# A fused attention, attention and mixture-of-experts kernel: six of eight expert matrices moved to the third phase, and its one-hot products in bf16

## The chip, the core and the metric

The kernel runs on one core of one Trainium2 chip. The metric is the device time of one execution in microseconds (us). The kernel before the change took 5177.51 us (median of 3 runs, 5173.71 to 5183.84).

A core has five engines that work side by side, each through its own queue in order: PE (TensorE, matrix products), DVE (VectorE), ACT (ScalarE), POOL (GpSimd) and SP (SyncE, which here only starts transfers). They wait for each other by semaphores. PE writes its results to PSUM[...].

## The reference, cut to what matters

A layer over x of 8 x 1024 tokens of 256 numbers: a first attention within each token (16 heads of 64, causal over the 64), a residual and a norm; then a second block with an ordinary attention over the leading axis, a norm giving y, and a mixture of experts:

```python
cap = S // E                                   # 8192 tokens, 8 experts: 1024
gates = softmax(xf @ wg); idx = argmax(gates)
loc = place of the token within its expert     # by a cumulative sum
keep = loc < cap
slot = idx * cap + loc
disp[slot] = xf
h = einsum('ecd,edf->ecf', disp, w1) + b1      # 256 -> 1024, no function between
y = einsum('ecf,efd->ecd', h, w2) + b2         # 1024 -> 256
out = where(keep, gate * y[slot], 0)
```

and two more norms. As nothing stands between w1 and w2, an expert is one matrix w1 w2 (256 x 256) and one bias row b1 w2 + b2. The kernel makes both itself, from inputs of 1 MB each per expert.

## The kernel before, in words

All work is in fp32 and in an order written out by hand (`tc.manual_schedule()`): each engine gets its instructions in the order in which the program calls them. There are three phases.

**Phase a** (`phase_a`) is the attention within tokens, over 64 tiles of 128 tokens. It takes the first 4332 us or so and isn't touched.

**Phase b** (`phase_b`, L540 on) is the attention over the leading axis and the choice of the expert. The tokens go in eight groups j of 1024. A group has four parts n. In part n, PE makes the `scores` of one half of the heads and one half of the positions; ACT turns them into `weights`; PE turns the result (`turn_s`) and makes the weighted sum of the part before. Between these steps the kernel calls the jobs of a list, `fills(j)`: the projections of the next group (`turn_x`, `project_qk`, `project_v`), and of the group before its `output`, `normal`, `turn_y`, `logits`, `exps` and `choice`. `some(k)` takes k jobs off the list, so the place of a job in the list decides what it stands between.

One kind of job is `expert(j, piece)` (L832): in group j the matrix of expert j is made, a quarter in each part. A piece is four fp32 products of 128x128 by 128x256 (L841), which accumulate in one PSUM bank `pw` over the four pieces, and two steps of DVE (L849) that add b1 times w2 to `acc`, from which the bias row comes. After the fourth piece ACT copies the bank to `w12` (L853). Each part's 256 KB of w1 and of w2 are started by SP at the start of the part (`load_expert`, L824), from a pool with two buffers each. SP's queue also holds the stores of finished rows (L765, L817) and the loads of x (L597).

`normal` makes y and y plus the bias of the second norm: two steps of DVE (L758), then three passes of POOL (L761, L762) to the tile `yx`; `turn_y` on PE (L773) waits for that. In group 7 there is no next group, and the expert's first piece stands earlier in the list.

**Phase c** (`phase_c`, L948 on) begins with the routing: PE counts with triangular and full matrices of ones (L975, L977, and `p_over`, L993), DVE works out each token's slot (split in `high` and `low`). Then one-hot products invert the list: for 8 columns of tokens at a time, DVE makes `is_low` (128 x 8 x 128) and `is_high` (128 x 8 x 64), POOL multiplies `is_high` with the token's number (L1056), and PE sums 64 products into `p_tok` (L1059). DVE casts the sum to `token`, the number of the token in each slot (L1063). The first row gather needs it.

Then come rounds r from -2 to 17 over 16 groups q of 512 slots. In round r, by the list `order`: POOL starts the gathers of q = r + 2 (L1083); ACT makes `roots`; PE turns the rows of q = r + 1 (`turned`, L1097) and ACT copies them to `xT` (L1101); PE makes the products of q = r + 1 with `w12` of its expert (`product`, L1108 and L1118); DVE adds them up for q = r (`blend`, L1147, L1135); ACT norms (`normed`, L1186: n of q = r - 1, o of q = r - 2); DVE adds the residual for q = r - 1 (`join`, L971); POOL scatters o of q = r - 2 to the output (L1204). Expert e is needed by the products of q = 2e and 2e + 1.

Of the kernel before, what the change touches and what calls it, by code (L numbers as in the profile page):

```python
# [24 lines left out]
FP = mybir.dt.float32  # L25
BF = mybir.dt.bfloat16
I32 = mybir.dt.int32
# [6 lines left out]
P = 128  # L34
D = 256
# [7 lines left out]
FC = FF // P  # L43
CAP = L * N // E
RW = 2 * D + 1
EPS = 1e-5
MASKED = 1e30

@with_exitstack
def fused_kernel(ctx: ExitStack, tc: tile.TileContext, a: dict, out: bass.AP):  # L50
    nc = tc.nc

    const = ctx.enter_context(tc.tile_pool(name="const", bufs=1))
    small = ctx.enter_context(tc.tile_pool(name="small", bufs=4))

    ident = const.tile([P, P], FP, name="ident")
    make_identity(nc, ident)
    mhalf = const.tile([P, 1], FP, name="mhalf")
    nc.gpsimd.memset(mhalf, -0.5)

    dram = ctx.enter_context(tc.tile_pool(name="dram", bufs=1, space=bass.MemoryType.DRAM))
    x1_d = dram.tile([L * N, D], FP, name="x1_d")
    rows_d = dram.tile([L * N, RW], FP, name="rows_d")

    def norm_scalars(r):

        st = small.tile([P, 6], FP, name="st")
        nc.vector.bn_stats(out=st, in_=r)
        mv = small.tile([P, 2], FP, name="mv")
        nc.vector.bn_aggr(out=mv, in_=st)  # L70
# [17 lines left out]
    constants(nc, late, keep)  # L88
    nc.scalar.dma_start(keep["gain"], a["ln2_g"].partition_broadcast(P))
    phase_b(tc, a, ident, x1_d, rows_d, keep, norm_scalars)  # L90
    phase_c(tc, ident, rows_d, keep, out)


def constants(nc, late, keep):
# [445 lines left out]
def phase_b(tc, a, ident, x1_d, rows_d, keep, norm_scalars):  # L540
# [8 lines left out]
    with (  # L549
# [271 lines left out]
            nc.vector.tensor_reduce(red_v[:, j], lg, AX.X, ALU.max)  # L821
            nc.vector.tensor_tensor(hot_v[:, j], rank, over_experts(red_v[:, j]), ALU.is_equal)

        def load_expert(e, piece):  # L824
            f0 = piece * 2 * P
            w1 = kp.tile([P, 2, D], FP, name="w1")
            nc.sync.dma_start(w1, a["w1T"][e, f0 : f0 + 2 * P, :].rearrange("(c p) d -> p c d", p=P))
            w2 = kp.tile([P, 2, D], FP, name="w2")
            nc.sync.dma_start(w2, a["w2"][e, f0 : f0 + 2 * P, :].rearrange("(c p) d -> p c d", p=P))
            G["we", e, piece] = w1, w2  # L830

        def expert(e, piece):  # L832

            w1, w2 = G["we", e, piece]
            if piece == 0:
                G["pw", e] = p1.tile([P, 512], FP, name="pw")
            pw = G["pw", e]
            for i in range(2):
                fc = piece * 2 + i
                for d in range(DC):  # L840
                    nc.tensor.matmul(  # L841
                        pw[:, d * D : (d + 1) * D],
                        w1[:, i, d * P : (d + 1) * P],
                        w2[:, i, :],
                        start=fc == 0 and d == 0,
                        stop=fc == FC - 1,
                        skip_group_check=True,
                    )
                nc.vector.scalar_tensor_tensor(  # L849
                    acc[:, e, :], w2[:, i, :], b1[:, fc, e : e + 1], acc[:, e, :], ALU.mult, ALU.add  # L850
                )
            if piece == 3:
                nc.scalar.copy(w12[:, :, e, :], pw.rearrange("p (c d) -> p c d", c=DC))  # L853

        def fills(j):

# [2 lines left out]
            nxt, prv = j + 1, j - 1  # L859
            N = nxt < NJ  # L860
            O = prv >= 0
            X = 0 <= j < NJ

            def put(part, ok, fn, *args):
                if ok:
# [2 lines left out]
            put(0, N, turn_x, nxt, 0)  # L868
            put(0, N, turn_x, nxt, 2)
            put(0, N, turn_x, nxt, 4)  # L870
            put(0, not N and X, expert, j, 0)
            put(0, O, output, prv, 0)
            put(0, N, turn_x, nxt, 6)
            put(0, O, output, prv, 2)
            put(0, N and X, expert, j, 0)
            put(0, O, normal, prv, 0)
            put(0, N, project_qk, nxt, 0, 0, 0)
            put(1, O, normal, prv, 2)
# [3 lines left out]
            put(1, O, logits, prv, 0)  # L882
            put(1, O, normal, prv, 4)
            put(1, O, turn_y, prv, 2)
            put(1, X, expert, j, 1)
# [8 lines left out]
            put(2, X, expert, j, 2)  # L894
# [8 lines left out]
            put(3, X, expert, j, 3)  # L903
            put(3, N, project_qk, nxt, 1, 1, 0)
            put(3, O, choice, prv)
            put(3, N, project_qk, nxt, 1, 1, 1)
            return o

        before = None
        for j in range(-1, NJ + 1):  # L910
# [4 lines left out]
            for n in range(4):  # L915
                work = list(parts[n])

                def some(k):
                    for _ in range(k):

                        if work and not (n == 0 and before and work[0][0] is output):
                            fn, *args = work.pop(0)
                            fn(*args)

                live = 0 <= j < NJ
                if live:
                    load_expert(j, n)
                    c, ib = divmod(n, 2)
                    st = scores(j, c, ib)
                    some(1)  # L930
                    weights(st, 0)
                if before:
                    sT = turn_s(before[3])
                    some(2 if live else 0)
                if live:
                    weights(st, 1)
                    normed(st)
                if before:
# [9 lines left out]
def phase_c(tc, ident, rows_d, keep, out):  # L948


    nc = tc.nc
# [3 lines left out]
    with (  # L955
        tc.tile_pool(name="cone", bufs=1) as op,
        tc.tile_pool(name="cwork", bufs=4) as kp,
        tc.tile_pool(name="crow", bufs=5) as gp,
        tc.tile_pool(name="cnorm", bufs=3) as np_,
        tc.tile_pool(name="cp", bufs=3, space=PSUM) as pp,  # L960
        tc.tile_pool(name="cq", bufs=4, space=PSUM) as pq,
        tc.manual_schedule(),
    ):
# [5 lines left out]

        def tt(o, x, y, alu):  # L970
            nc.vector.tensor_tensor(o, x, y, alu)  # L971


        p_in = pp.tile([P, 512], FP, name="ps")
# [17 lines left out]
        p_over = pp.tile([P, 512], FP, name="ps")  # L992
        nc.tensor.matmul(p_over[:, :NT], keep["before"], over, start=True, stop=True)  # L993
        nc.tensor.matmul(p_over[:, NT : 2 * NT], keep["ones"], over, start=True, stop=True)
        tt(slot, slot, loc, ALU.add)

        count = new("count", (P, E))
# [36 lines left out]
        nc.vector.scalar_tensor_tensor(low, high, -float(P), slot, ALU.mult, ALU.add)  # L1034


        K = 8
        p_tok = pq.tile([P, 512], FP, name="pr")
        column = keep["column"]
        for k in range(NT // K):  # L1040
            ts = slice(K * k, K * k + K)
            is_low = np_.tile([P, K, P], FP, name="is_low")
            tt(
                is_low,
                low[:, ts, None].to_broadcast([P, K, P]),
                column[:, None, :].to_broadcast([P, K, P]),
                ALU.is_equal,
            )
            is_high = np_.tile([P, K, NT], FP, name="is_high")
            tt(  # L1050
                is_high,
                high[:, ts, None].to_broadcast([P, K, NT]),
                column[:, None, :NT].to_broadcast([P, K, NT]),
                ALU.is_equal,
            )
            nc.gpsimd.tensor_tensor(is_high, is_high, place[:, ts, None].to_broadcast([P, K, NT]), ALU.mult)  # L1056
            for i in range(K):
                t = K * k + i
                nc.tensor.matmul(  # L1059
                    p_tok[:, :NT], is_low[:, i, :], is_high[:, i, :], start=t == 0, stop=t == NT - 1  # L1060
                )
        token = op.tile([P, NT], I32, name="token")
        nc.vector.tensor_copy(token, p_tok[:, :NT])  # L1063

        valid = new("valid", (P, E, ST))
        tt(
            valid,
# [2 lines left out]
            ALU.is_lt,  # L1070
        )
        valid = valid.rearrange("p e s -> p (e s)")

        st = {}
        moments = {}
# [123 lines left out]
        def scatter(q, i):  # L1199
# [21 lines left out]
            (turned, -1, 1),  # L1221
            (product, -1, 0),
            (product, -1, 1),
            (blend, 0, 0),
            (scales, None),
            (normed, 1, 0),
# [9 lines left out]
        for r in range(-2, NQ + 2):  # L1236
            for fn, d, *args in order:
                if d is None:
                    fn(r)
# [48 lines left out]
```

## Time and profile before

| what | value |
|---|---|
| median of 3 runs | 5177.51 us |
| the profiled execution, its own time | 5169.03 us |
| its span, first to last instruction | 5167.3 us |
| PE busy over the span | 4927.5 us, 95% |
| DVE, ACT, POOL busy | 59%, 65%, 65% |
| mean granted clock of PE | 0.976 |
| expert products, L841 | 256 instructions, 67.2 us busy |
| bias steps, L849 | 64 instructions, 43.2 us busy |
| one-hot products, L1059 | 128 instructions, 27.6 us busy |
| POOL's multiply, L1056 | 8 instructions, 10.1 us busy |

An fp32 product counts as two instructions of PE in the profile, so 128 products of L841 are 256. A row of the timeline gives the start in us from the start of the span, the time that it lasts, the engine (PEld is PE's loading of weights), the line, the operation, output and inputs with shapes, how many instructions were merged (x8), and in brackets the idle time of the engine just before it and what ended that. The granted clock is the share of full speed at which PE was allowed to run. Several rows of one line follow each other closely: an instruction may start before the end of the one before it, so the price of one in a row is the distance of the starts.

### The profile page before, as it was taken

The page shows a single profiled execution, that of the slowest core. Times are in us where ns is not written, and L with a number is a line of the kernel's source. Part 1 is how long each engine was busy: PE and PEld are TensorE (multiplying, and loading weights), DVE is VectorE, ACT ScalarE, POOL GpSimd, SP SyncE. Part 2 cuts the span into 40 slices and gives each one's busy share as a digit, 9 for nine tenths or more (in the row PEclk, how much of TensorE's full clock was granted, in tenths as well). Part 3 has the DMA queues.
Part 4 walks back from the last instruction along what each step waited for, and adds up shares of the span by engine and source line. Part 5 has one row for each costly group of instructions (what it writes and reads, how often), then busy time and mean ns, then how long its engine had stood idle before and what let it go on. Part 6 is the DMA issues. An engine that isn't in the chain of part 4 may idle for free. (4 is left out here: it accounts for less than half of the span.)

```text
span 5167.3 us, 189788 instructions
## 1 busy us (share of the span) xinstructions
PE 4927.5 (95%) x79752; PEld 3334.8 (65%) x79752; DVE 3065.7 (59%) x6079; ACT 3348.2 (65%) x4067; POOL 3377.5 (65%) x7022
## 2 busy tenths in 40 slices
PE   7999999999999999999999999999999997998765
PEld 4666666666666666666666666666666664666553
DVE  5656666566656666656656566656666652555467
ACT  5777777777777777777777777777777773443224
POOL 5767666767676776667667767676776763344446
PEclk9999999999999999999999999999999998999877
DMA  2222222222222222222222222222222222233223
GB/s 76 47 48 49 47 49 48 47 47 48 49 47 47 48 49 46 48 48 49 47 48 49 47 48 49 48 47 48 48 49 46 48 47 72 62 82 82 62 81 120
DMA packets 569357, 280.00 MB, mean 54 GB/s; under 512 B 395057, under 2 KB 520113, under 8 KB 568497
## 3 DMA queue, kind: packets, MB, share of 16 engines
q1 hardware_dynamic: 360018, 105.22, 10.8%
q0 software_dynamic: 204800, 159.82, 10.5%
q8 instruction: 623, 10.21, 0.9%
q10 hardware_dynamic: 3680, 2.83, 0.2%
q14 instruction: 236, 1.93, 0.1%
HBM read 66.02 MB, written 33.59 MB: 19 GB/s over the span
## 5 line engine op out<-in xcount | busy, mean ns | idle before, releaser
L358 ACT ACTIVATE e<-pair 128x1024 f32<-128x1024 f32 x3072 | 2977.3, 1021 | 1235.5 <-PE pair L342 1235.5
L402 POOL DMA_DIRECT2D nd<-S x4096 | 1948.9, 484 | 612.0 <-DVE S L392 418.8
L342 PE MATMUL pair<-R,L 32*128 32x128 f32 (+1 forms) x32768 | 1606.2, 322 | 2.2 <-POOL event L313 2.1
L392 DVE COPY S<-sum 128x512 f32<-128x512 f32 x1024 | 706.6, 690 | 1469.2 <-PE sum L381 1138.7
L342 PEld LDWEIGHTS pair<-R,L 32*128 32x128 f32 x32768 | 1271.7, 186 | 48.9 <-POOL event L313 3.4
L372 PE MATMUL sum<-e,V 128*32 128x256 f32 x16384 | 1285.7, 385 | 4.9 <-DVE S L392 4.9
L299 POOL DMA_DIRECT2D R<-qm x2048 | 973.7, 483 | 73.3 <-issue 40.1
L381 PE MATMUL sum<-e,V 128*32 128x128 f32 x16384 | 823.9, 273 | 0.0
L381 PEld LDWEIGHTS sum<-e,V 128*32 128x32 f32 x16384 | 533.2, 110 | 352.6 <-issue 1.6
L372 PEld LDWEIGHTS sum<-e,V 128*32 128x32 f32 x16384 | 406.5, 109 | 236.6 <-DVE qm L266 41.8
L330 PE MATMUL pair<-late,sel 32*128 32x256 bf16 (+1 forms) x6144 | 499.4, 313 | 9.6 <-ACT e L358 9.6
L253 DVE COPY V<-vT 32x128 f32<-32x128 f32 x2048 | 456.4, 223 | 28.1
L330 PEld LDWEIGHTS <-sel 32*128 32x128 bf16 x6144 | 155.4, 91 | 460.6 <-issue 445.2
L411 DVE RECIPROCAL att<-nd 128x256 f32<-128x256 f32 x256 | 447.3, 1747 | 7.1 <-DMA nd<-S 3.2
L313 POOL MEMSET event<- 1x1 f32 x256 | 22.6, 88 | 618.2 <-DMA R<-qm 402.4
L233 PEld LDWEIGHTS ps<-xT,wv 128*128 128x128 f32 x2048 | 238.2, 191 | 44.4 <-issue 41.8
L222 PE MATMUL ps<-wk,xT 128*128 128x512 f32 x512 | 255.7, 622 | 11.6 <-DMA wk<-in_Wk 10.8
L233 PE MATMUL ps<-xT,wv 128*128 128x128 f32 x2048 | 262.6, 281 | 1.6 <-DVE qm L266 0.8
L265 PE MATMUL ps<-wq,xT 128*128 128x512 f32 x512 | 255.7, 622 | 5.7 <-DVE k L223 5.7
L442 PE MATMUL ps<-wo,attT 128*128 128x256 f32 x1024 | 257.2, 394 | 0.7 <-ACT attT L425 0.7
L72 POOL TENSOR_SCALAR ve<-mv 128x1 f32<-128x1 f32 x128 | 37.5, 293 | 313.3 <-DVE mv L70 311.9
L442 PEld LDWEIGHTS ps<-wo,attT 128*128 128x128 f32 x1024 | 185.6, 191 | 63.4 <-issue 41.8
(185 smaller groups left out, 3893.0 us busy)
## 6 DMA issues: line engine op xcount, KB each, us to landing
R<-qm POOLq DMA_DIRECT2D x2048, 32.0 KB, 2.1
nd<-S POOLq DMA_DIRECT2D x4096, 16.0 KB, 1.9
L<-k SPq DMA_DIRECT2D x4088, 8.0 KB
rows_d<-yx SPq DMA_DIRECT2D x32, 512.0 KB
xT<-in_xT SPq DMA_DIRECT2D x64, 128.0 KB
xr<-in_x SPq DMA_DIRECT2D x64, 128.0 KB
x_d<-x1o SPq DMA_DIRECT2D x64, 128.0 KB
x<-x_d SPq DMA_DIRECT2D x8, 1024.0 KB
```

The source lines that it names most:

```text
L233: nc.tensor.matmul(ps[:, i * P : (i + 1) * P], w["v"][:, c, ch * P : (ch + 1) * P], xT_of[t][:, c, :], start=c == 0, stop=c == DC - 1,)
L253: nc.vector.tensor_copy(V[32 * aa : 32 * aa + 32, qd % 2, :, qd // 2, :, aa, 0:4], src[32 * qd : 32 * qd + 32, :, ww, :, aa, :],)
L299: moved.append((None, nc.gpsimd.dma_start(R[:, b, s, b, :], q[:, b, s, cols])))
L330: nc.tensor.matmul(bank[u].rearrange("p (n i) -> p n i", i=n)[:, :, 0:32], sel[pr].rearrange("p a j -> p (a j)"), late[pr, None, :].to_bro ...
L342: one = nc.tensor.matmul(bank[u][:, x * 4 * n : (x + 1) * 4 * n].rearrange("p (b i) -> p b i", i=n), Lt[pr, 2 * (h0 + h) + jb].rearrange(" ...
L358: nc.scalar.activation(e, pair[i], AF.Exp)
L372: nc.tensor.matmul(dst[32 * u : 32 * u + 32], Vs[ww][:, 0, h0 + h, u, :], e0[u // 2][:, u % 2, x * 256 : (x + 1) * 256].rearrange("p (b i) ...
L381: nc.tensor.matmul(dst[32 * u : 32 * u + 32, :, 32:], Vs[ww][:, 1, h0 + h, u, :], e1[u // 2][:, u % 2, h * 128 : (h + 1) * 128].rearrange( ...
L392: nc.vector.tensor_copy(S[:, :, 2 * which : 2 * which + 2, :].rearrange("p b h i -> p h b i"), ps.rearrange("p (h b i) -> p h b i", h=2, b=4),
L402: nc.gpsimd.dma_start(tok[:, b, s, h0 * C1 : (h0 + G) * C1], Sx[:, 4 if s else b, b, :])
L411: nc.vector.reciprocal(att[:, cols], nd[:, 1, cols])
L442: nc.tensor.matmul(ps[:, :D], attT[:, c, :], wo[:, c, :], start=c == 0, stop=c == HID // P - 1)
```

## The change

In phase b only the bias steps of experts 2 to 7 remain, in the places where the whole pieces were, in groups 0 to 5, with loads of w2 alone. Experts 0 and 1 are made in group 7, two pieces at the end of each part, with the first two loads one group earlier. The six others are made in phase c from loads of a whole expert (two of 1 MB, three buffers each): expert 2 after `p_over`, expert 3 in eight pieces between the one-hot chunks, expert 4 after the token, and experts 5 to 7 with two products of fc (four of PE) in each of the rounds -2 to 9. ACT copies each finished expert from a bank of its own.

The one-hot tiles become bf16. The sum over p + 128 t is split into two columns of sums, one with p and one with t: ACT scales `is_high` by p for all columns and by t for six columns of eight, DVE by t for the other two. PE makes 64 products of 128x128 by 128x128. DVE then joins the two sums to the token. POOL's multiply goes, and `valid` is made before the one-hot loop instead of after.

```diff
-        def load_expert(e, piece):
+        def load_expert(e, piece, w1=True):
             f0 = piece * 2 * P
...
+            for n in ("w1", "w2") if w1 else ("w2",):
...
+            expert_bias(e, piece)
             if piece == 3:
                 nc.scalar.copy(w12[:, :, e, :], pw.rearrange("p (c d) -> p c d", c=DC))
+            following = 4 * e + piece + 2
+            if following < 4 * EARLY:
+                load_expert(*divmod(following, 4))
...
-            X = 0 <= j < NJ
+            X = 0 <= j < E - EARLY
...
-            put(0, not N and X, expert, j, 0)
...
-            put(0, N and X, expert, j, 0)
+            put(0, X, expert_bias, EARLY + j, 0)
...
+            if j == NJ - 1:
+                for n in range(4):
+                    for i in range(EARLY):
+                        k = EARLY * n + i
+                        put(n, True, expert, *divmod(k, 4))
...
-                    load_expert(j, n)
+                    if j < E - EARLY:
+                        load_expert(EARLY + j, n, False)
+                    if j == NJ - 2 and n > 1:
+                        load_expert(0, n - 2)
```

In phase c:

```diff
+        def load(e):
+            if e < E:
+                ex[e] = [xp.tile([P, FC, D], FP, name=n) for n in ("w1", "w2")]
+                for tile_, n in zip(ex[e], ("w1T", "w2")):
+                    nc.sync.dma_start(tile_, a[n][e].rearrange("(c p) d -> p c d", p=P))
+
+        def expert(e, fc):
+
+            w1, w2 = ex[e]
+            if fc == 0:
+                ex["w", e] = pw.tile([P, DC * D], FP, name="pw")
+            ps = ex["w", e]
+            for d in range(DC):
+                nc.tensor.matmul(
+                    ps[:, d * D : (d + 1) * D],
+                    w1[:, fc, d * P : (d + 1) * P],
+                    w2[:, fc, :],
...
+            if fc == FC - 1:
+                nc.scalar.copy(keep["w12"][:, :, e, :], ps.rearrange("p (c d) -> p c d", c=DC))
+                load(e + 3)
...
+        for e in range(EARLY, EARLY + 3):
+            load(e)
...
+        some(FC)
         tt(slot, slot, loc, ALU.add)
...
+            is_low = np_.tile([P, K, P], BF, name="is_low")
...
+            is_high = np_.tile([P, K, NT], BF, name="is_high")
...
-            nc.gpsimd.tensor_tensor(is_high, is_high, place[:, ts, None].to_broadcast([P, K, NT]), ALU.mult)
+            both = np_.tile([P, K, 2, NT], BF, name="both")
+            nc.scalar.activation(both[:, :, 0, :], is_high, AF.Copy, scale=place[:, 0:1])
+            for i in range(KD, K):
+                nc.scalar.activation(both[:, i, 1, :], is_high[:, i, :], AF.Copy, scale=float(K * k + i))
+            few = slice(K * k, K * k + KD)
+            tt(
+                both[:, :KD, 1, :],
+                is_high[:, :KD, :],
+                column[:, few, None].to_broadcast([P, KD, NT]),
+                ALU.mult,
+            )
...
+                    p_tok[:, : 2 * NT],
+                    is_low[:, i, :],
+                    both[:, i].rearrange("p s h -> p (s h)"),
...
+            some(1)
...
+        nc.vector.scalar_tensor_tensor(token, parts[:, NT:], float(P), parts[:, :NT], ALU.mult, ALU.add)
+        some(FC)
...
             (product, -1, 1),
+            (some, None, 2),
             (blend, 0, 0),
```

More of the change, by code (lines that the diff above doesn't have):

```diff
@@ L45 @@
 RW = 2 * D + 1
+EARLY = 2
 EPS = 1e-5
@@ L90, in fused_kernel @@
     phase_b(tc, a, ident, x1_d, rows_d, keep, norm_scalars)
-    phase_c(tc, ident, rows_d, keep, out)
+    phase_c(tc, a, ident, rows_d, keep, out)
 def constants(nc, late, keep):
@@ L822, in choice @@
             nc.vector.tensor_tensor(hot_v[:, j], rank, over_experts(red_v[:, j]), ALU.is_equal)
-        def load_expert(e, piece):
+        def load_expert(e, piece, w1=True):
             f0 = piece * 2 * P
[L826 to L830, printed above, removed]
+            G["we", e, piece] = []
+            for n in ("w1", "w2") if w1 else ("w2",):
+                w = kp.tile([P, 2, D], FP, name=n)
+                src = a["w1T" if n == "w1" else n][e, f0 : f0 + 2 * P, :]
+                nc.sync.dma_start(w, src.rearrange("(c p) d -> p c d", p=P))
+                G["we", e, piece].append(w)
         def expert(e, piece):
@@ L848, in expert, with expert_bias @@
                     )
-                nc.vector.scalar_tensor_tensor(
-                    acc[:, e, :], w2[:, i, :], b1[:, fc, e : e + 1], acc[:, e, :], ALU.mult, ALU.add
-                )
+            expert_bias(e, piece)
             if piece == 3:
                 nc.scalar.copy(w12[:, :, e, :], pw.rearrange("p (c d) -> p c d", c=DC))
+            following = 4 * e + piece + 2
+            if following < 4 * EARLY:
+                load_expert(*divmod(following, 4))
+        def expert_bias(e, piece):
+            for i in range(2):
+                fc = piece * 2 + i
+                nc.vector.scalar_tensor_tensor(
+                    acc[:, e, :], G["we", e, piece][-1][:, i, :], b1[:, fc, e : e + 1], acc[:, e, :], ALU.mult, ALU.add
+                )
         def fills(j):
@@ L884, in fills @@
             put(1, O, turn_y, prv, 2)
-            put(1, X, expert, j, 1)
+            put(1, X, expert_bias, EARLY + j, 1)
             put(1, N, project_v, nxt, 0)
@@ L893, in fills @@
             put(2, O, normal, prv, 6)
-            put(2, X, expert, j, 2)
+            put(2, X, expert_bias, EARLY + j, 2)
             put(2, N, project_v, nxt, 2)
@@ L902, in fills @@
             put(3, O, exps, prv)
-            put(3, X, expert, j, 3)
+            put(3, X, expert_bias, EARLY + j, 3)
             put(3, N, project_qk, nxt, 1, 1, 0)
@@ L945, in phase_b, with phase_c @@
                     load_x(j + 2)
-def phase_c(tc, ident, rows_d, keep, out):
+def phase_c(tc, a, ident, rows_d, keep, out):
     nc = tc.nc
@@ L959, in phase_c @@
         tc.tile_pool(name="cnorm", bufs=3) as np_,
+        tc.tile_pool(name="cexp", bufs=3) as xp,
         tc.tile_pool(name="cp", bufs=3, space=PSUM) as pp,
+        tc.tile_pool(name="cw", bufs=1, space=PSUM) as pw,
         tc.tile_pool(name="cq", bufs=4, space=PSUM) as pq,
@@ L971, in tt, with some @@
             nc.vector.tensor_tensor(o, x, y, alu)
+        ex = {}
+        def load(e):
[13 more added lines that the diff above has]
+                    w2[:, fc, :],
+                    start=fc == 0 and d == 0,
+                    stop=fc == FC - 1,
+                    skip_group_check=True,
+                )
+            if fc == FC - 1:
+                nc.scalar.copy(keep["w12"][:, :, e, :], ps.rearrange("p (c d) -> p c d", c=DC))
+                load(e + 3)
+        pieces = [(e, fc) for e in range(EARLY, E) for fc in range(FC)]
+        def some(k):
+            for _ in range(k):
+                if pieces:
+                    expert(*pieces.pop(0))
+        for e in range(EARLY, EARLY + 3):
+            load(e)
         p_in = pp.tile([P, 512], FP, name="ps")
@@ L1034, in phase_c @@
         nc.vector.scalar_tensor_tensor(low, high, -float(P), slot, ALU.mult, ALU.add)
[L1037 to L1055, printed above, removed]
-            nc.gpsimd.tensor_tensor(is_high, is_high, place[:, ts, None].to_broadcast([P, K, NT]), ALU.mult)
[L1057 to L1063, printed above, removed]
         valid = new("valid", (P, E, ST))
@@ L1072, in phase_c @@
         valid = valid.rearrange("p e s -> p (e s)")
+        K, KD = 8, 2
+        p_tok = pq.tile([P, 512], FP, name="pr")
+        column = keep["column"]
+        for k in range(NT // K):
+            ts = slice(K * k, K * k + K)
+            is_low = np_.tile([P, K, P], BF, name="is_low")
+            tt(
+                is_low,
+                low[:, ts, None].to_broadcast([P, K, P]),
+                column[:, None, :].to_broadcast([P, K, P]),
+                ALU.is_equal,
+            )
+            is_high = np_.tile([P, K, NT], BF, name="is_high")
+            tt(
+                is_high,
+                high[:, ts, None].to_broadcast([P, K, NT]),
+                column[:, None, :NT].to_broadcast([P, K, NT]),
+                ALU.is_equal,
+            )
+            both = np_.tile([P, K, 2, NT], BF, name="both")
[3 more added lines that the diff above has]
+            few = slice(K * k, K * k + KD)
+            tt(
+                both[:, :KD, 1, :],
+                is_high[:, :KD, :],
+                column[:, few, None].to_broadcast([P, KD, NT]),
+                ALU.mult,
+            )
+            for i in range(K):
+                t = K * k + i
+                nc.tensor.matmul(
+                    p_tok[:, : 2 * NT],
+                    is_low[:, i, :],
+                    both[:, i].rearrange("p s h -> p (s h)"),
+                    start=t == 0,
+                    stop=t == NT - 1,
+                )
+            some(1)
+        token = op.tile([P, NT], I32, name="token")
+        parts = new("parts", (P, 2 * NT))
+        nc.vector.tensor_copy(parts, p_tok[:, : 2 * NT])
+        nc.vector.scalar_tensor_tensor(token, parts[:, NT:], float(P), parts[:, :NT], ALU.mult, ALU.add)
+        some(FC)
         st = {}
@@ L1238, in phase_c @@
                 if d is None:
-                    fn(r)
+                    fn(*args or (r,))
                 elif 0 <= r - d < NQ:
```

## The prediction

> **What bounds the kernel now.** I read the page first (PE busy 95%), then the busy time by stage, because the change touches only the last 850 us: phase b (4332 to 4922, eight groups of about 64 us and two ends) and phase c (routing to 4968, then rounds). Columns: stretch, its length, busy us of PE, weight loads, DVE, ACT, POOL, then granted clock, DMA share, GB/s.
>
> ```profile
> core 0: us, PE busy (x) PEld busy (x) DVE busy (x) ACT busy (x) POOL busy (x), PEclk, DMA share, GB/s
> 4500.00:4580.00 80.00, 71.34 (x436) 52.25 (x435) 44.21 (x98) 32.19 (x107) 40.36 (x47) 0.94 0.36 86
> 4922.00:4940.00 18.00, 4.22 (x8) 1.73 (x7) 13.97 (x34) 0.00 (x0) 1.74 (x1) 0.59 0.00 0
> 4940.00:4968.00 28.00, 27.57 (x128) 27.38 (x128) 12.94 (x15) 0.00 (x0) 8.33 (x8) 0.50 0.00 1
> 5040.00:5090.00 50.00, 40.54 (x140) 27.67 (x140) 46.19 (x135) 26.22 (x53) 39.72 (x59) 0.83 0.51 151
> ```
>
> Phase b is bound by PE, the routing by DVE and then by the one-hot products (PE full at half clock), the rounds by DVE (46 of 50). So PE work moved from b to c leaves a bound engine for one with room. Next the timeline of one group, to see which of its four expert pieces (L841) really stand on the path:
>
> ```profile
> 4561.68 1.89 PE L841 MATMUL pw<-w,w 128*128 128x256 f32 x8
> ...
> 4570.58 1.11 PE L773 MATMUL fill<-ident,yx 128*128 128x128 f32 x4 [3.06 <-POOL yx L761]
> ...
> 4571.49 3.62 PE L741 MATMUL fill<-wout,oT 128*128 128x256 f32 x8
> ...
> 4579.89 1.89 PE L841 MATMUL pw<-w,w 128*128 128x256 f32 x8
> ```
>
> The piece at 4561.68 is followed, 9 us later, by a wait for POOL; the pieces at 4579.89, 4594.11 and 4609.90 lie in a stretch where PE never waits, except for the weights of the last. Group 7 and the block of ACT:
>
> ```profile
> 4817.92 3.75 PE L841 MATMUL pw<-w,w 128*128 128x256 f32 x8 [6.03 <-DMA w<-in_w]
> ...
> 4874.85 0.59 ACT L853 COPY w<-pw 128x512 f32<-128x512 f32 x1 [4.86 <-PE pw L841]
> ```
>
> The second row is the one to remember: the copy of a finished expert stands in ACT's queue and waits 4.86 us for PE. Last, the end of routing and one round:
>
> ```profile
> 4967.78 0.22 DVE L1063 CAST token<-pr 128x64 int32<-128x64 f32 x1 [8.41 <-PE pr L1059]
> ...
> 5052.91 2.07 ACT L1186 ACTIVATE n<-z,nm,rs 128x256 f32<-128x256 f32 x4 [1.45 <-DVE nm L1178]
> ...
> 5055.02 1.23 DVE L971 TENSOR_TENSOR n<-n,gain 128x1024 f32<-128x1024 f32 x1
> ...
> 5055.81 1.89 PE L1118 MATMUL pr<-w,xT 128*128 128x256 f32 x8
> ```
>
> A round is 10.38 us. ACT's four n end, and DVE's join starts at once; PE ends the products of the round at 5057.7, 2.7 us after that join began.
>
> **Phase b, groups 0 to 6.** A piece lasts 1.89 us in its row, but the next instruction starts 1.73 us after it (4561.68 to 4563.41): 1.73 is what its removal frees. Piece 0 frees nothing: in group 0 a 3.45 us wait for DVE's xT follows it, in groups 1 to 6 the wait for yx, whose chain (r, the moments, POOL's three passes) doesn't contain it. The wait grows from 3.06 to 4.8 us. Pieces 1 to 3 are on the path: 7 groups x 3 x 1.73 = 36.3. With them go the waits for the weights before piece 3 (0.91, 0.57, 0.52, 1.18, 2.17 in groups 1 to 5): 5.4; and two pieces that ran slow (2.46 and 3.32 for 1.89): 2.0. I checked what is late next: turn_y of parts 2 and 3 has its yx 2.9 us early each, and 1.2 and 1.1 us are left after the shifts. The w2 of part 3 lands some 7 us behind the 1 MB x load and is then wanted about when it lands, hidden by 3 us of idle DVE before the next mx. DVE's bias steps stay where they were. Sum 43.7.
>
> Here a rule speaks against the change. The Trainium skill, "TensorE: Matmul & The Clock Gate", section "HAM oscillation — how this bites in real kernels", says that gaps of over about 3.4 us put PE back to half clock. By it the wait of 3.06 would be free and that of 4.8 not: at the price of the 3.62 us row plus its neighbours, some 2.9 us in each of six groups, 17 in all. But the row shows the 3.62 (1.89 elsewhere) after only 3.06: the price is already paid. I take 0, and keep up to 6 for a longer slow spell.
>
> **Group 7.** Before, its expert stands ahead of turn_s, waits 6.03 for weights and runs at half clock: output 0 starts at 4825.9, and without it could start at 4818.0, 7.9 earlier. After, two pieces stand at the end of each part, their weights loaded one part ahead. PE has waits of 3.1 to 3.2, 2.4 and 2.5 us there, but eight bias steps on DVE (0.94 each beside POOL, by the row of 1.88 for two) stand before the next mx, and cost about 1 in part 1, 1.9 in parts 2 and 3. Net -4 (between -1.6 and -7). **Phase b: -48 (-40 to -52).**
>
> **Routing.** All numbers here on the old clock of phase c.
> - Loads on SP: 12 x 1 MB; nothing but each other is queued behind them. The first three experts wait for the last buffers of b, at the latest the gate's store (issued 4920.5, its traffic over by 4922.2). At 350 GB/s, what the rows at 4348 to 4354 moved, 2 MB take 6 us: expert 2 at about 4931, just when PE ends p_over (4931.1). If only the 197 to 256 GB/s of 4602 to 4606 (x load and w) held, it would be 4934.
> - Expert 2 on PE: 32 instructions at 0.213, 6.8 us, 9 with a cold start: to 4940. ACT's copy waits for it, and the first one-hot ACTIVATE stands behind that copy: 4941.
> - DVE per chunk of 8 columns: is_low 1.14 and is_high 0.61 start to start (no row has fp32 in and bf16 out; the inputs stay, so I take the same price, and were it half, ACT would still be the bound), the new product of 128 columns about 0.25: 2.05. POOL's multiply (8 x 1.26) goes. valid moves ahead: 0.2.
> - ACT per chunk: no row for a bf16 copy. 128x512 lies at 0.58 to 0.69 (L777, L625), 128x64 at 0.26 alone (L806), about 0.2 in a row (128x128 follow at 0.25). So 1.5 to 2.3, I take 1.8, by the rows where several follow each other. ACT ends at 4941 + 8 x 1.8 = 4955.4, DVE at 4953.
> - PE: 64 products in one bf16 pass of 128 columns. No row; between 0.1 and 0.2 each with the load (L330 loads bf16 in 0.09), 1.6 a chunk at most, and a piece of expert 3, 0.43 to 0.87. Under 2.05 while the clock is full.
> - token at 4956 (4955 to 4960) for 4968.0: -12. But not all of it arrives: PE then makes expert 4 (a copy's gap 0.8, 6.8), another gap 0.8, and the two pieces of round -2 (1.7): free at 4966.4. The four gathers, started 4956.5, 1.27 apart and 3.6 long, landed at 4964; expert 6's load beside them may cost 2.
>
> **Rounds.** Each of the 12 rounds -2 to 9 gets four products, 1.73. PE per round: 0.9 turned + 5.2 products + 1.7 = 7.8 of 10.4; hidden. The price is ACT's copy of experts 5, 6, 7, in rounds 1, 5, 9. It stands behind the xT copies and **ahead of n** (the instruction order shows it), and waits for the products and pieces of its own round. Behind it: n, then DVE's join, and o, the scatter and the last gather.
> - Round 1: from 4966.4, rounds -1, 0 and 1 take PE 3 x 7.8 = 23.4, to 4989.8; copy to 4990.5, four n to 4992.6: the first join starts where it did before (4992.84). The whole gain of the token is spent here: -0.2 (-4 to +6).
> - Rounds 5 and 9: PE's products end 0.9 (full clock) to 2.7 after the old start of the join, + 1.7 pieces + 0.6 copy + 2.1 n: the join is 5.5 to 7.3 late, and the DVE-bound loop cannot win it back: 2 x 6.2 = +12.4.
> **Phase c: +12 (+4 to +20).**
>
> **Sum.** -48 + 12 = -36. The profiled execution took 5169.0 (span 5167.3), so such a one would take 5133. The median of the three runs, 5177.5, lies 8.5 above it; I take the same difference for the changed kernel: 5177.5 - 36 = 5142.
>
> **Rivals.**
> - The copy doesn't hold: PE ends rounds 5 and 9 early enough for n. For it: PE's clock rises with more work. Against: even at full clock 5.5 us are late. Then c is about 0 or a little below, with b at its best: -60 to -48, 5117 to 5129. Chance 0.13.
> - A cold phase c: the granted clock was 0.50 to 0.59 in routing. If expert 2, the chunks and expert 4 run at half clock, token comes at 4962, PE is free 14 us later, round 1 starts late: c at +28, net -20, 5157. Against: PE is now dense from 4931. Chance 0.17.
> - Slower: PE becomes the bound of the rounds. At half clock a round costs 15.6 instead of 10.4, 11 rounds give +57, with 12 and -48 net +21: 5199. It turns the sign where the clock in the rounds is under 0.57 (11 x (7.8/c - 10.4) = 36). The row has 0.83 with less work. Chance 0.03.
> - The change doesn't pay: the groups are bound by the yx chains throughout and PE's freed time becomes waits; only the 5.4 of waits and group 7 are left: +2 to +7, 5180 to 5184. Against: PE never waits in parts 1 to 3. Chance 0.05.
> - My forecast: 0.62, own range 5128 to 5156 (both stage ranges half used).
>
> Range 5118 to 5160. A measurement of this kernel can tell 0.2% (10 us) from no change. Faster 0.92, same 0.04, slower 0.04.
>
> **What would show it.** Group period 58 for 64 us, with the wait before turn_y at 4.8. The token at some 35 us after the start of routing (4921.6) instead of 46, with DVE and ACT, not PE, as the last before it. An ACT wait of about 5 us at the copy in rounds 5 and 9, and DVE idle before the join there. Wrong if the period falls by over 7 (piece 0 did count) or under 4, if a load holds expert 2 beyond 4934, or if rounds 5 and 9 last 10.4.

## The result and the profile after

The changed kernel takes 5144.52 us (median of 4 runs, 5141.15 to 5145.15); the kernel before took 5175.61 us in the runs beside it. The ratio is 0.9936, with a 95% interval of 0.9918 to 0.9953: 31 us faster. The profiled execution took 5145.15 us, its span is 5143.4 us, its mean granted clock 0.977. Profile against profile the gain is only 23.9 us, because the profiled execution of before lay 6.6 us under that median and the one of after 0.6 us above its own.

First the busy time by stage of the kernel after, with the columns of the table in the prediction. The stretches are the start of the routing, the one-hot chunks, and 50 us of rounds.

```profile
4881.00:4899.00 18.00, 8.31 (x17) 5.22 (x18) 13.80 (x36) 0.00 (x0) 0.00 (x0) 0.59 0.69 219
4899.00:4921.00 22.00, 20.04 (x120) 15.34 (x118) 13.39 (x22) 13.33 (x58) 0.00 (x0) 0.96 0.64 203
5020.00:5070.00 50.00, 34.78 (x140) 25.07 (x141) 41.09 (x123) 23.45 (x48) 35.72 (x53) 0.91 0.44 135
```

The chunks now run at a clock of 0.96 where it was 0.50. The last row shows a loss: DVE, the bound of the rounds, was busy 46 of 50 us and is now busy 41; something makes it wait.

Next the timeline of PE in one group of phase b. The first expert piece stood just ahead of the first row, and is gone:

```profile
4549.93 1.96 PE L623 MATMUL fill<-xT,wi 128*128 128x512 f32 x4 [0.63 <-DVE xT L612]
...
4558.06 1.11 PE L774 MATMUL fill<-ident,yx 128*128 128x128 f32 x4 [3.93 <-POOL yx L762]
4558.96 3.62 PE L742 MATMUL fill<-wout,oT 128*128 128x256 f32 x8
```

Its 1.73 us became waits: 0.63 for xT, 0.87 more before turn_y (3.93 for 3.06), and 0.2 between. The groups 1 to 6 last 57.8 to 58.1 us each, from the first scores of one to those of the next (63.5 to 66.8 before). Then the routing, in the rows of ACT, DVE and SP:

```profile
4879.81 0.36 SPq L818 DMA_DIRECT2D rows_d<-gate  x1
4886.32 0.37 SPq L999 DMA_DIRECT2D w<-in_w1T  x1
...
4895.08 9.99 PE L1008 MATMUL pw<-w,w 128*128 128x256 f32 x32 [4.84 <-DMA w<-in_w]
...
4905.10 0.59 ACT L1017 COPY w<-pw 128x512 f32<-128x512 f32 x1 [26.32 <-PE pw L1008]
4905.58 0.72 ACT L1127 ACTIVATE both<-is_high,place 128x512 bf16<-128x512 bf16 x1
...
4907.48 1.22 DVE L991 TENSOR_TENSOR is_low<-low,column 128x1024 bf16<-128x1024 f32 x1 [5.77 <-PE pr L1139]
...
4919.88 0.23 DVE L1150 SCALAR_TENSOR_TENSOR token<-parts 128x64 int32<-128x64 f32 x1
```

This is a chain to be read downward. SP starts expert 2's load only 6.5 us after the gate's store, PE waits 4.84 us for it, ACT's copy waits for PE, and the first one-hot step of ACT stands behind that copy. DVE, which had made three chunks ahead, then idles 5.77 us, until PE has used the first. The token is done 39.2 us after the start of the routing (4880.92), where it was 46.4.

Last, a round that ends an expert (round 5):

```profile
4989.15 1.23 DVE L991 TENSOR_TENSOR n<-n,gain 128x1024 f32<-128x1024 f32 x1
...
5002.29 0.59 ACT L1017 COPY w<-pw 128x512 f32<-128x512 f32 x1 [6.31 <-PE pw L1008]
5002.77 2.07 ACT L1265 ACTIVATE n<-z,nm,rs 128x256 f32<-128x256 f32 x4
5004.88 1.23 DVE L991 TENSOR_TENSOR n<-n,gain 128x1024 f32<-128x1024 f32 x1 [5.42 <-ACT n L1265]
```

The joins are 15.7 us apart instead of 10.4. ACT waited 6.31 us for PE at the copy of expert 6, n waited behind it, and DVE waited 5.42 us for n. Round 9 is the same (15.8).

### The profile page after: what moved, and what is told of

Same layout as the page of the kernel before. It is cut to its first block, busy times and chain, and to the rows that moved or that the text cites. A ratio compares the mean times of both kernels' runs of the same rounds, so it can differ in the third digit from the quotient of the medians.

```text
span 5143.4 us, 189684 instructions
## 1 busy us (share of the span) xinstructions
PE 4903.2 (95%) x79688; PEld 3310.9 (64%) x79688; DVE 3070.0 (60%) x6088; ACT 3360.9 (65%) x4123; POOL 3374.4 (66%) x7014
## 3 DMA queue, kind: packets, MB, share of 16 engines
q0 software_dynamic: 204800, 159.82, 10.4%
## 5 line engine op out<-in xcount | busy, mean ns | idle before, releaser
L300 POOL DMA_DIRECT2D R<-qm x2048 | 973.8, 483 | 71.7 <-issue 39.2
```

The lines of the kernel that those rows point to most:

```text
L300: moved.append((None, nc.gpsimd.dma_start(R[:, b, s, b, :], q[:, b, s, cols])))
```

## The experiments

**The theory** had three parts: in phase b, pieces 1 to 3 are on PE's path and piece 0 is not; in the routing, expert 2's late load holds ACT; in the rounds, ACT's copy holds the join. The rivals are given with each run. Three chips were used, one for each group of four runs; the kernel before was run beside each, so ratios are compared across groups, and times within one.

**Phase c, four runs on one chip** (before: 5177.61 us).

The copies put behind the norm steps:

```diff
             if fc == FC - 1:
+                done.append((e, ps))
+                if e < 5:
+                    copied()
+                load(e + 3)
+
+        done = []
+
+        def copied():
+            while done:
+                e, ps = done.pop()
                 nc.scalar.copy(keep["w12"][:, :, e, :], ps.rearrange("p (c d) -> p c d", c=DC))
-                load(e + 3)
...
             (normed, 2, 1),
+            (late_copy, None),
```

> The changed kernel, but ACT copies experts 5, 6 and 7 behind the eight norm steps (n and o) of their rounds instead of ahead of them. Theory A (the copy, standing in ACT's order ahead of n, holds the join): rounds 5 and 9 fall from 15.7 to 10.4 us, which is -10.7, and the first join comes earlier by the 6.2 us of waiting and 0.6 of copying at most, at least by 3: 5127 to 5131 us, where the changed kernel took 5144.5. Rival B (PE's products and pieces of these rounds hold the join on another way too, so the wait only moves to DVE or to the xT copies): rounds 5 and 9 stay over 13 us and the time within 5 us of 5144.5.

Measured: 5127.75 us, ratio 0.9906 (0.9891 to 0.9921). The joins of this kernel about round 5, and the copy in its new place:

```profile
4992.96 1.23 DVE L991 TENSOR_TENSOR n<-n,gain 128x1024 f32<-128x1024 f32 x1
4997.26 0.59 ACT L1027 COPY w<-pw 128x512 f32<-128x512 f32 x1 [2.37 <-PE pw L1008]
5003.34 1.23 DVE L991 TENSOR_TENSOR n<-n,gain 128x1024 f32<-128x1024 f32 x1
```

ACT still waits 2.37 us at the copy, and no join waits for it: the joins are 10.38 apart. The first join stands 68.7 us after the start of the routing instead of 76.9; 1.6 us of that are the token, which came earlier in this execution, and 6.6 come behind the token, where ACT had waited 6.21 us at the copy of expert 5. Theory A holds: an instruction moved by a few places in one queue is worth some 16 us (15.5 by the two ratios, 17.3 by the trace without the token's 1.6).

Expert 2 loaded early:

```diff
+    keep["e2"] = [late.tile([P, FC, D], FP, name=n) for n in ("e1", "e2")]
...
+                if j == NJ and n == 0:
+                    for tile_, m in zip(keep["e2"], ("w1T", "w2")):
+                        nc.sync.dma_start(tile_, a[m][EARLY].rearrange("(c p) d -> p c d", p=P))
...
-        for e in range(EARLY, EARLY + 3):
+        ex[EARLY] = keep["e2"]
+        for e in range(EARLY + 1, EARLY + 4):
```

> The changed kernel, but expert 2 has tiles of its own, which are loaded some 50 us earlier (at the start of the last part of phase b), so that its load waits for no store of the gate. Theory A (expert 2 comes late from memory, so PE makes it late, so ACT's copy holds the first one-hot step, and DVE idles 5.8 us): PE makes expert 2 without a wait for a transfer, DVE's idle time in the chunks goes, the token comes 34 us instead of 39.2 after the start of routing, and the first join moves with it: 5144.5 - 5.5 = 5139. Rival B (after the token the gathers beside the loads of experts 6 and 7 decide): the token is earlier and the first join isn't: 5143 to 5145.

Measured: 5141.51 us, ratio 0.9932 (0.9918 to 0.9945). In this kernel PE needs no transfer for expert 2, and ACT is free 5 us earlier:

```profile
4890.79 9.30 PE L1012 MATMUL pw<-e,e 128*128 128x256 f32 x32
4900.13 0.59 ACT L1021 COPY w<-pw 128x512 f32<-128x512 f32 x1 [20.98 <-PE pw L1012]
...
4914.91 0.22 DVE L1156 SCALAR_TENSOR_TENSOR token<-parts 128x64 int32<-128x64 f32 x1
```

The routing starts at 4881.29, so the token is done after 33.8 us, and the first join comes after 71.5 instead of 76.9. The chain of the routing is as told. Of the 5.3 us of the first join the median shows 3, and the intervals of the two ratios overlap, so the size rests on the trace. The trace also shows where a part went in this execution: round 5 lasts 17.3 us here and not 15.7, because one row of its products ran at half speed:

```profile
4990.93 3.49 PE L1203 MATMUL pr<-w,xT 128*128 128x256 f32 x8
```

That row takes 1.89 us in the changed kernel, and ACT's copy stands behind it.

Both together:

> Both edits: expert 2 loaded early into tiles of its own, and the copies of experts 5 to 7 behind the norm steps. Theory A (the two holds stand one behind the other): the gains add up, 5144.5 - 5.5 - 16 = 5123. Rival B (they overlap ahead of the first join, because both only shift when ACT gets to the first n, and PE's expert 4 and the gathers then decide): only the larger counts there, 5128 to 5133.

Measured: 5122.43 us, ratio 0.9896 (0.988 to 0.9911). The first join stands 64.5 us after the start of the routing, and the later ones 10.3 to 10.5 apart (8.4 the last). The two holds stood one behind the other and add up. Phase c lasts 239.2 us, from the start of the routing to the end of the span, where it was 245.7 with no expert in it and 262.5 in the changed kernel.

The loads of experts 6 and 7 left out:

```diff
-            if e < E:
+            if e in (6, 7):
+                ex[e] = ex[5]
+            elif e < E:
```

> The changed kernel without the loads of experts 6 and 7: their products are made from the tiles of expert 5 instead, so the matrices of experts 6 and 7 are those of expert 5. Theory A (the 4 MB stand beside the first gathers, whose last transfer took 7.1 us for 3.6 before, but PE is busy with expert 4 until 4930.8 and waits only 0.5 for the rows): 5143.5 to 5144.5. Rival B (the slow gathers put off the first rounds, and that is the part of the first join's lateness): gathers at 3.6 us again and the first join 3 to 5 us earlier, 5140 to 5141.5.

Measured: 5146.19 us, ratio 0.9942 (0.9928 to 0.9955). The first twelve gathers in the listing of DMA issues (the last number is the median of us from issue to landing), first of the changed kernel:

```profile
g<-rows_d,token POOLq DMA_INDIRECT x12, 6.8
```

and then of this one:

```profile
g<-rows_d,token POOLq DMA_INDIRECT x12, 3.7
```

The gathers do land 3.1 us sooner, and it buys little. From the token to the first join 36.8 us pass instead of 37.7, because PE is busy with expert 4 and the two pieces behind it until 4930.8 anyway. The runs without products and without bias steps (below) keep these loads and need 36.9 and 37.5, so even this 0.9 us is not clear. The execution loses more in round 5, which lasts 17.4 us with a slow row of products, as with expert 2 loaded early. The slow landing is real and nearly off the path.

**Parts of the change alone, four runs on another chip** (before: 5214.14 us; on this chip single rounds last 16 us or more; ACT's copy of the turned rows waits up to 17 us there, for something that the traces don't name; phase b is as on the others).

Only the one-hot part on the kernel before:

> The kernel before with only the one-hot part of the change: bf16 tiles, p and t apart, ACT scales, valid ahead of the loop; all eight experts stay in phase b. Theory A (PE's fp32 products at half clock held the token, then DVE's 2.06 us a chunk does): the token 34.5 us instead of 46.4 after the start of routing, and since no expert stands between the token and the rounds, the first join earlier by nearly as much: 5177.6 - 11.5 = 5166. Rival B (PE is half cold in the first rounds, and the rounds' start is held by it, not by the token): the first join only 4 to 6 us earlier, 5172.

Measured: 5200.37 us, ratio 0.9976 (0.9967 to 0.9985), 13.8 us faster. Its routing starts at 4921.24, and this is its token:

```profile
4954.81 0.23 DVE L1091 SCALAR_TENSOR_TENSOR token<-parts 128x64 int32<-128x64 f32 x1
```

The token is done after 33.8 us, 12.6 earlier than before. The first join comes after 67.9 us; in the two runs below, which share the chip and have the old routing, it comes after 83.8 and 78.7. So theory A holds, and the gain reaches the end. The bf16 part is worth its 12 us (7.8 to 17 by the interval, on this chip) as long as no expert is put around it.

Piece 0 left out of seven groups:

```diff
-                for d in range(DC):
+                for d in range(DC if piece != 0 or e == 7 else 0):
...
-                        start=fc == 0 and d == 0,
+                        start=fc == (0 if e == 7 else 2) and d == 0,
```

> The kernel before without the products of piece 0 in groups 0 to 6 (so the matrices of experts 0 to 6 lack a quarter of their sum; loads, bias steps and copies stay). Theory A (PE waits for yx behind it anyway): no gain, 5175 to 5178, the wait before turn_y 4.8 for 3.06 us. Rival B (the yx chain begins behind that piece, at the output or at DVE's r, so it shifts along): a gain of up to 7 x 1.73 = 12.1 us, 5165.5, and the wait stays at 3.06; the changed kernel's wait of 3.9 would give half of it, 5171.

Measured: 5214.02 us, ratio 0.9997 (0.9989 to 1.0006). Nothing, as forecast. The row of turn_y in this kernel:

```profile
4570.57 1.12 PE L773 MATMUL fill<-ident,yx 128*128 128x128 f32 x4 [3.92 <-POOL yx L761]
```

It starts 19.7 us after the first scores of its group, as before. With a wait of 0.62 for xT ahead of it, this is the picture of the changed kernel: two chains, xT's and yx's, take up the 1.73 us between them.

Piece 1 left out, in the same way:

> The kernel before without the products of piece 1 in groups 0 to 6 (again a quarter of seven matrices is left out). Theory A (this piece stands in a stretch where PE never waits): 7 x 1.73 = 12.1 us earlier, 5165.5. Rival B (the freed time turns into waits at turn_y of parts 2 and 3, whose yx comes from POOL): under 6 us, 5172 or more.

Measured: 5200.53 us, ratio 0.9975 (0.9965 to 0.9985), 13.6 us faster for 12.1 expected (7.8 to 18 by the interval). So a piece counts by its place. Pieces 2 and 3 were not left out singly. One group differs: group 0 lasts 47.55 us in this run and 47.44 without piece 0, against 47.58 with all pieces. There neither piece is on the path.

The bias steps of group 7 behind the maximum:

```diff
-            expert_bias(e, piece)
...
+            behind.append((e, piece))
...
                     st = scores(j, c, ib)
+                    biases()
```

> The changed kernel, but the bias steps of experts 0 and 1 in group 7 stand on DVE behind the maximum of the next part's scores instead of ahead of it, and the next loads of weights behind them. Theory A (the four steps of 3.8 and 4.7 us hold that maximum 4.2 us in part 1 and 2.4 us in part 3, and PE waits for sT): group 7 gains 2.4 to 6 us, 5138.5 to 5142 where the changed kernel took 5144.5. Rival B (the missing gain went to PE, whose pieces of 16 products take 5.7 and 6.7 us for 3.6 at a lower clock, and to POOL's yx and xb): within 1.5 us of 5144.5.

Measured: 5191.11 us, ratio 0.9957 (0.9943 to 0.997). The total is not to be compared with the 0.9936 of another chip; the stage is: group 7 lasts 64.05 us instead of 66.3, from the first scores to the last weighted sum. That is 2.2 less, below theory A's span of 2.4 to 6 and above rival B's 1.5. But the four runs of phase c have group 7 unedited, and there it lasts 65.6, 65.6, 63.8 and 65.3 us: a gain of 2.2 is no more than this spread. The shortest of these groups is also the one in which PE needs least for the products of experts 0 and 1, 17.3 us where the changed kernel needs 19.5. So this run decides nothing.

**Group 7 and the best version, four runs on a third chip** (before: 5174.77 us).

The changed kernel itself, unedited:

> The changed kernel once more, as the measure for the other three on their chip: 0.9936 of the kernel before, and group 7 (first scores to last weighted sum) 65.3 to 66.3 us, as in its earlier runs; before, 67.1.

Measured: 5147.9 us, ratio 0.9945 (0.9931 to 0.9959), 27 us faster where the first result was 31; the intervals overlap. Group 7 lasts 66.28 us, up to the start of its last weighted sum.

Without the products of experts 0 and 1:

```diff
-                for d in range(DC):
+                for d in range(DC if fc == FC - 1 else 0):
...
-                        start=fc == 0 and d == 0,
+                        start=d == 0,
```

> The changed kernel without the products of experts 0 and 1 in group 7, but for the last of the eight steps of each (the two matrices lack seven eighths of their sum; loads, bias steps and copies stay). Theory A (the prediction: these pieces lie for the most part in waits of PE): group 7 is 2 to 4 us shorter. Rival B (they stand on PE's path, ahead of the scores of the next part, at a lower clock, and this is where the missing gain of group 7 went): 8 to 14 us shorter.

Measured: 5143.97 us, ratio 0.9939 (0.9925 to 0.9952); group 7 lasts 62.46, 3.8 us less than in the changed kernel beside it and 1.3 less than in the shortest unedited one (63.8). Theory A holds against rival B's 8 to 14: of the 15.4 us of PE that go (19.5 in the changed kernel's rows, 4.1 are left), at most 3.8 show, and the rest becomes waits. The first turn_y, first in the changed kernel on this chip:

```profile
4794.63 1.12 PE L774 MATMUL fill<-ident,yx 128*128 128x128 f32 x4 [3.02 <-POOL yx L762]
```

and then in this one:

```profile
4793.28 1.11 PE L774 MATMUL fill<-ident,yx 128*128 128x128 f32 x4 [6.47 <-POOL yx L762]
```

It starts 21.6 us after the group's first scores in both.

Without the bias steps of experts 0 and 1:

```diff
-            expert_bias(e, piece)
             if piece == 3:
```

> The changed kernel without the bias steps of experts 0 and 1 in group 7 (their bias rows lack b1 times w2; products, loads and copies stay). Theory A (the bias steps hold the maximum in parts 1 and 3): group 7 is 3 to 6 us shorter. Rival B (PE and POOL set the end of these parts): under 2 us shorter, as with the bias steps put behind the maximum.

Measured: 5142.28 us, ratio 0.9939 (0.9925 to 0.9953); group 7 lasts 61.68, 4.6 us less than beside it and 2.1 less than the shortest unedited one. That is inside theory A's 3 to 6 when taken from the run beside it: the bias steps do cost time in group 7, up to 4.6 us. These are the bias steps of the changed kernel in its part 0, and the maximum behind them, whose scores PE had ended at 4787.7:

```profile
4788.18 3.82 DVE L862 SCALAR_TENSOR_TENSOR acc<-w,b,acc 128x256 f32<-128x256 f32 x4
4791.93 1.21 DVE L680 TENSOR_REDUCE mx<-sc 128x8 f32<-128x1024 f32 x1
```

The maximum starts 4.2 us after its scores are done, and the bias steps are 3.75 of that; in part 3 (4.70 us of bias steps) it is 2.4 late. That the time goes by way of the maximum isn't shown: with the steps behind it group 7 is no shorter than the spread of unedited runs allows.

All three edits together:

> Expert 2 loaded early into its own tiles, the copies of experts 5 to 7 behind the norm steps, and the bias steps of group 7 behind the maximum. Theory A: 0.9896 of the kernel before, as with the first two alone, less 1 to 2 us of group 7: 0.9892. Rival B (the 2 MB for expert 2 or the later loads of weights take it back): 0.9896 or more.

Measured: 5120.24 us, ratio 0.9895 (0.9879 to 0.991); group 7 lasts 63.28. With or without the third edit (0.9896) is the same within the interval. This version is faster than both kernels: 1.05% below the kernel before.

## Why the prediction was right, point by point

The forecast was 5142, the measurement is 5144.5. The mechanism was right in both phases, but several terms were too hopeful, and the nearness is in part luck. By the two profiles phase b gave 40.7 us for 48 and phase c cost 16.8 for 12. That makes 23.9 instead of 36, an execution of 5145 for 5133. Of the 40.7, 42.4 are won in the groups below; 1.2 is lost because phase b begins later in the profiled execution of after, by the spread of phase a, which wasn't touched, and 0.5 behind group 7. What closed the gap is the last step of the sum, "I take the same difference for the changed kernel": the 8.5 us between profiled execution and median are the spread of single executions, and here the changed kernel's difference is 0.6 the other way.

**Groups 1 to 6: right.** 39.1 us for 38.5. That piece 0 frees nothing and piece 1 its 1.73 is shown by leaving out each; for pieces 2 and 3 the length of the groups speaks. The wait before turn_y is 3.9, not 4.8: the rest waits for xT. The rule in "TensorE: Matmul & The Clock Gate", section "HAM oscillation — how this bites in real kernels", of the Trainium skill, that gaps over some 3.4 us bring half clock, would have cost up to 17 us more; the trace shows the same 3.62 us row behind the wait of 3.9 as behind 3.06. Taking 0 was right.

**Group 0: wrong place in the sum.** The term "7 groups x 3 x 1.73" has one group too many. Group 0 has no group before it to fill PE with; leaving out one piece there gives nothing, and the whole change gave 2.5 us for 5.2.

**Group 7: mechanism right, size off.** The net was 0.8 us for 4 in these two profiles. Other executions with the same group 7 gave up to 3.3 (63.8 for 67.1), so a part of the miss is the spread of executions. Two terms carry the rest. "Could start at 4818.0, 7.9 earlier": the outputs started 7.2 us after the group's first scores for 14.4, so that came true, but they ran in 5.7 us for 4.1, and turn_y of part 1 was only 5.8 earlier (21.6 us after the first scores for 27.4). And from there to the last weighted sum the group takes 5.0 us longer, where the net of 4 allowed 3.9. A bias step costs 0.96 to 1.18 us where POOL is at work, not 0.94, and the holds were put in the wrong parts: "about 1 in part 1, 1.9 in parts 2 and 3" was taken, and the maximum is 4.2 late in part 1, not at all in part 2, and 2.4 in part 3.

**Token: mechanism right, size off.** DVE's chunk at 2.05 us was right (2.06; the three terms that the prediction names add to 2.00, and is_high takes 0.72 start to start for its 0.61), and is_low with bf16 output costs 1.13 start to start, as taken. ACT's chunk costs 1.48 us when it is not held (1.8 taken), so DVE is the bound. The gain was 7.2 us for 12, because the term "expert 2 at about 4931" was 4.8 us too early, counted from the start of the routing: it took SP to start the load when the store's traffic was over, 1.7 us after the store's start, but SP went on 6.5 us after the store's start. From there to PE's first weights it took 8.8 us, which is what the forecast left between 4922.2 and 4931 (its own 6 us for 2 MB would have given 4928). PE then took 10.0 us for 9. On the prediction's clock the weights came at 4935.8. A load that holds expert 2 beyond 4934 was one of its signs of being wrong, so this one came true. With the load made early the token is where it was forecast, 33.8 us for 34.4.

**First join: size off with it.** +5.6 us for -0.2, inside the range of -4 to +6, near its end. Between the token and the first join 37.7 us passed, and 36.6 were forecast: most of the lateness is that of the token. That this join is held by the copy was in the prediction, and the run with the copies behind shows it.

**Rounds 5 and 9: right.** +10.7 us for +12.4, by the wait that was named. The lower price is PE's full clock (1.00 granted from 4984 to 5005), which the prediction gave as the lower end: 5.5 a round, and its terms add to 5.3, where 5.3 and 5.4 were measured. The rivals "the copy doesn't hold" and "PE becomes the bound of the rounds" fall with it. Of "a cold phase c" only expert 2's start was seen.

What stays open: group 7 without bias steps and without products is up to 4.6 and 3.8 us shorter, one at a time; how much of the two is the same time wasn't tried. Why SP's load waits 6 us for a store of 4 KB the runs don't show, nor what ACT waits for in the 16 us rounds of the one chip.

## What to carry to other kernels

Work that is moved to an engine with room brings instructions for other engines along, and these go into in-order queues: for each, ask what stands behind it, and put it behind the step that the bound engine waits for; here that was worth half as much as the whole change. A product on a busy engine counts by its place: leaving out one of two equal pieces gave 0.1 us, leaving out the other 13.6. A load into memory that another stage still holds may start well after the traffic of that stage's last store is over, here 4.9 us; giving the first load memory of its own took that wait off the path.

## What the runs showed of the hardware

- A store of 4 KB in 1040 packets held SP's next load: 6.5 us from its issue to the issue of the load behind it (6.0 to 6.4 in three other runs), of which the trace puts 5.8 down to that store. Its traffic was over after 1.6 us.
- ACT makes six bf16 copies of 128x64 in 0.97 us in a row, and one of 128x512 in 0.72. DVE gains nothing from a bf16 output with fp32 inputs here: 1.22 us for 128x1024 and 0.68 for 128x512, and 1.23 and 0.69 with fp32 output.
- Twelve gathers land in 6.8 us (median) beside loads, with 326 to 413 GB/s moved in all, and in 3.7 alone.
- A bias step on DVE (128x256, fp32) takes 0.51 us where POOL stands still (four in 2.04 us at 4831.5 of the changed kernel), and 0.96 to 1.18 where POOL is at work.
- Without piece 0, two groups ran longer, 68.2 and 66.2 us for 64 to 66: PE's piece 3 took 3.75 and 3.64 us for 1.97 there, behind waits for weights of 1.74 and 1.02. A wait of 1.79 in the run without piece 1 left it at 1.97. Half speed after a short wait is not a matter of that wait alone.
